# Who evicts the turned normal rows, and where GpSimd's centring stands in its queue, in a fused encoder-decoder kernel

## The chip, the cores and the metric

The kernel runs on one core of a Trainium2 chip. The metric is the device time of one execution in microseconds; the time of a kernel is the median of its runs. A core has a matrix engine (TensorE, in the profile PE, its weight loads PEld), a vector engine (VectorE, DVE), an engine for activation functions (ScalarE, ACT), a general engine (GpSimd, POOL) and one that issues the DMAs here (SyncE, SP). Each engine works through its own queue in program order and waits for the others at semaphores. [...]

## What is computed

One encoder layer over a short context (2 x 77 rows) and one decoder layer over the input (2 x 2048 rows, width 512, 16 heads of 32), both with a normalization ahead of each part. All is in fp32. The reference, cut to the part that matters here:

```python
yn = _ln(y, dec_n1_s, dec_n1_b)                    # (x - mean) * rsqrt(var + eps) * s + b
y = y + _mha(yn, yn, dec_sa_in_w, dec_sa_in_b, dec_sa_out_w, dec_sa_out_b, sb)    # causal, relative bias
y = y + _mha(_ln(y, dec_n2_s, dec_n2_b), memory, ...)                             # cross attention
h = _ln(y, dec_n3_s, dec_n3_b)
y = y + (relu(h @ dec_ff1_w.T + dec_ff1_b) @ dec_ff2_w.T + dec_ff2_b)
```

## The kernel before

The self attention comes first and takes the span up to about 1745 us; cross attention and feed forward of all blocks follow. The self attention goes through 8 blocks of 512 rows (2 sequences, `b`, by 4, `m`). A block has 16 units: 4 groups `g` of 4 heads by 4 tiles `t` of 128 rows. A unit's scores reach over `m * 4 + t + 1` tiles of keys, so units of the first block of a sequence (`m` = 0) are short, and those of the last are long.

For every unit the main loop (lines 1479 to 1504) does this, in program order of all engines: `scores` (L372 on TensorE, the maxima on VectorE in L381 and L388, their combination `nm` in L398, the exponentials on ScalarE in L403), `turn` (L426: TensorE transposes the probabilities into PSUM banks, which L432 on ScalarE and L430 on VectorE copy out), and `values` (L443). Where a unit ends, three lists are worked through for the next unit `n + 1`: first `ahead[n + 1]`, before the last `turn` of unit `n`; after that `turn`, in `slot(n + 1)`, `light`, then the projections of `jobs`, then `late`. The lists are filled by hand in lines 935 to 968. In the first blocks `late` also carries the encoder's stages (L584 to L633), and `light` the first cross attention's stages in the fifth and sixth block (L764 to L853).

The part at hand is the normalization of the rows of the next block, one tile of 128 rows at a time, while a block is worked on:

- `norm_load` (L272) loads the tile.
- `norm_stats` (L277): mean and variance on VectorE (L281 to L284), then 1 / sqrt by GpSimd's power (L285).
- `norm_center` (L288): (x - mean) * rstd in place, on GpSimd (L292), for the very first block on VectorE.
- `norm_turn` (L294): four 128x128 transpositions on TensorE (L304) into one bank, then four evictions that apply scale and bias per partition, into `nT`, from which the next block's `q_job`, `k_job` and `v_job` read. For the first block `apart` is true: two banks, the first quarter evicted by VectorE (L311), the other three by ScalarE (L309). For the other seven blocks, 28 tiles, VectorE evicts all four quarters (L311).

The stages of tile `t` stand at the units 5 + t (load), 6 + t (statistics and centring) and 7 + t (turning) of the block before. In the same slots stand `residual` (a DMA, then GpSimd's add in L266, which waits for it), the stages of `spread` (GpSimd's multiply in L471) and `out_job` (L251 on TensorE, L254 on VectorE, which reads the residual of the unit before). In `light` they come ahead of the centring.

PSUM's banks 0 to 6 are handed out in turn by `bank()`: each user takes the next one, and TensorE's writing waits until the bank's last user, seven requests earlier, has been evicted. Bank 7 collects the values.

Of the kernel before, what the change touches and what calls it, by code (L numbers as in the profile page):

```python
# [54 lines left out]
def tile_encoder_decoder(ctx: ExitStack, tc: tile.TileContext, ins, out):  # L55
# [21 lines left out]
    def vec(name, i):  # L77
        c = _COL[name] + i
        return vecs[:, c : c + 1]
# [78 lines left out]
    with (  # L158
# [20 lines left out]
        def bank():  # L179

            i = count["bank"] % count["banks"]
            count["bank"] += 1
            return psum[:, i, :]
# [27 lines left out]
        def q_job(b, m, g):  # L211
            def run(w):
                mm = bank()
                for c in range(NC):
                    nc.tensor.matmul(mm, w[:, c, :], nTs[b, m][:, c, :], start=(c == 0), stop=(c == NC - 1))
                q = sb.tile([P, MB], F32, name="q", tag="q", bufs=3)
                nc.vector.tensor_scalar(q, mm, vec("dec_sa_in_b", g), SCALE, ALU.add, ALU.mult)
                qTs[b, m, g] = q

            return lambda: small_w(g * P), run, True  # L220

        def k_job(b, m, g):
            def run(w):
                mm = bank()
                for c in range(NC):
                    nc.tensor.matmul(mm, w[:, c, :], nTs[b, m][:, c, :], start=(c == 0), stop=(c == NC - 1))
                d, bi = kT[:, g, ts(m, MB)], vec("dec_sa_in_b", NC + g)
                if m >= 2:
                    nc.vector.tensor_scalar(d, mm, bi, None, ALU.add)
                else:  # L230
                    nc.scalar.activation(d, mm, AF.Identity, bias=bi)

            return lambda: small_w(D + g * P), run, True

        def v_job(b, m, t):
            def run(w):
                mm = bank()
                for c in range(NC):
                    nc.tensor.matmul(
                        mm, nTs[b, m][:, c, ts(t, P)], w[:, c, :], start=(c == 0), stop=(c == NC - 1)  # L240
                    )
                nc.vector.tensor_tensor(vv[:, m * TB + t, :], mm, bv, ALU.add)

            return lambda: big_w("v", b, m), run, False

        def out_job(b, m, t):
            def run(w):
                x1 = xr.pop((b, m, t))
                mm = bank()
                for c in range(NC):  # L250
                    nc.tensor.matmul(  # L251
                        mm, ots[b, m, c][:, ts(t, P)], w[:, c, :], start=(c == 0), stop=(c == NC - 1)
                    )
                nc.vector.tensor_tensor(x1, mm, x1, ALU.add)  # L254
                nc.sync.dma_start(y1[b][m][:, t, :], x1)

            return lambda: big_w("o", b, m), run, False
# [10 lines left out]
        def residual(b, m, t):  # L268
            residual_load(b, m, t)
            residual_add(b, m, t)  # L270

        def norm_load(b, m, t, place=None):  # L272
            x1 = sb.tile([P, D], F32, name="xt", tag="xt", bufs=2) if place is None else place
            nc.sync.dma_start(x1, x_rows[b, m, :, t, :])
            xs[b, m, t] = x1

        def norm_stats(b, m, t):  # L277
            x1 = xs[b, m, t]
            st = sm.tile([P, 6], F32, name="bnst", tag="bnst")
            mv = sm.tile([P, 2], F32, name="bnmv", tag="bnmv")  # L280
            nc.vector.bn_stats(st, x1)  # L281
            nc.vector.bn_aggr(mv, st)
            rs = sm.tile([P, 2], F32, name="rstd", tag="rstd")
            nc.vector.tensor_scalar_add(rs[:, 0:1], mv[:, 1:2], EPS)  # L284
            nc.gpsimd.tensor_tensor(rs[:, 1:2], rs[:, 0:1], mhalf[:, 0:1], ALU.pow)  # L285
            xs[b, m, t] = x1, mv, rs

        def norm_center(b, m, t):  # L288
            x1, mv, rs = xs[b, m, t]
            xs[b, m, t] = x1  # L290
            engine = nc.gpsimd if (b, m) != (0, 0) else nc.vector
            engine.tensor_scalar(x1, x1, mv[:, 0:1], rs[:, 1:2], ALU.subtract, ALU.mult)  # L292

        def norm_turn(b, m, t, apart=False):  # L294
            xn = xs.pop((b, m, t))
            if t == 0:
                nTs[b, m] = nTt
            nT = nTs[b, m]

            pts = [bank()] * NC  # L300
            if apart:
                pts[0] = bank()
            for c in range(NC):
                nc.tensor.transpose(pts[c][:, ts(c, P)], xn[:, ts(c, P)], ident)  # L304
            for c in range(NC):
                d, pt = nT[:, c, ts(t, P)], pts[c]
                sc, bi = vec("dec_n1_s", c), vec("dec_n1_b", c)
                if apart and c:
                    nc.scalar.activation(d, pt[:, ts(c, P)], AF.Identity, bias=bi, scale=sc)  # L309
                else:  # L310
                    nc.vector.tensor_scalar(d, pt[:, ts(c, P)], sc, bi, ALU.mult, ALU.add)  # L311
# [162 lines left out]
        def divide(b, m, g):  # L474


            ri = sm.tile([P, TB, HC], F32, name="ri", tag="ri", bufs=2)
            nc.vector.reciprocal(ri, sums_of[b, m, g])
            rows = sm.tile([P, TB, HC, HD], F32, name="rirows", tag="rirows", bufs=1)
            nc.vector.tensor_copy(rows, ri[:, :, :, None].to_broadcast([P, TB, HC, HD]))  # L480
            yield
            rb = bank()
            flat = rows.rearrange("p t r d -> p (t r d)")
            for t in range(TB):
                nc.tensor.transpose(rb[:, ts(t, P)], flat[:, ts(t, P)], ident)
            nc.vector.tensor_tensor(ots[b, m, g], rb, ots[b, m, g], ALU.mult)
            yield
# [440 lines left out]
        NU = NC * TB  # L928
        jobs = {n: [] for n in range(-1, len(units) + NU)}
        light = {n: [] for n in range(-1, len(units) + NU)}  # L930

        ahead = {n: [] for n in range(-1, len(units) + NU)}
        late = {n: [] for n in light}

        for x, (b, m) in enumerate(blocks):
            u = x * NU
            first = m == 0

            jobs[max(u - 5, -1)].append(q_job(b, m, 0))
            jobs[max(u - 4, -1)].append(k_job(b, m, 0))  # L940
            jobs[(u + 1 if first else u - 3 + (x == 1)) if x else -1].append(v_job(b, m, 0))
            jobs[(u + 2 if first else u - 2 + (x == 1)) if x else 1].append(v_job(b, m, 1))
            jobs[u + 3 if first else u + 1].append(v_job(b, m, 2))
            jobs[u + 4 if first else u + 2].append(v_job(b, m, 3))
            jobs[u - 1 if x else 0].append(q_job(b, m, 1))
            jobs[u if x else 2].append(k_job(b, m, 1))
            for g, at, then in ((2, 3, 4), (3, 5, 6)) if x else ((2, 3, 4), (3, 5, 6)):
                jobs[u + at].append(q_job(b, m, g))
                jobs[u + then].append(k_job(b, m, g))
            for t in range(TB):  # L950
                end = x == len(blocks) - 1
                jobs[u + NU + (2 if end else 7) + t].append(out_job(b, m, t))
                if not end:
                    light[u + NU + 6 + t].append(lambda b=b, m=m, t=t: residual(b, m, t))
                elif t < 2:
                    light[u + NU - 1].append(lambda b=b, m=m, t=t: residual(b, m, t))
                if x:
                    light[u - NU + 5 + t].append(lambda b=b, m=m, t=t: norm_load(b, m, t))
                    ahead[u - NU + 6 + t].append(lambda b=b, m=m, t=t: norm_stats(b, m, t))
                    light[u - NU + 6 + t].append(lambda b=b, m=m, t=t: norm_center(b, m, t))  # L960
                    light[u - NU + 7 + t].append(lambda b=b, m=m, t=t: norm_turn(b, m, t))
            for g in range(NC):
                apart = not (x == len(blocks) - 1 and g >= NC - 2)
                d = spread(b, m, g) if apart else divide(b, m, g)
                for k in range(4 if apart else 2):
                    light[u + g * TB + TB + k].append(lambda d=d: next(d, None))
                at = u + g * TB - 3
                light[max(at, -1)].append(lambda b=b, m=m, g=g: load_bias(b, m, g))
# [197 lines left out]
        u = 2 * NU  # L1166
# [5 lines left out]
        u = 6 * NU  # L1172
# [399 lines left out]
```

## Time and profile before

| what | us |
|---|---|
| median of 3 runs (2849.39 to 2850.22) | 2850.07 |
| the profiled execution's own time | 2851.01 |
| its span, first to last instruction | 2849.2 |
| TensorE busy in the span | 2800.5 |
| VectorE busy | 1888.1 |
| ScalarE busy | 1370.0 |
| GpSimd busy | 836.7 |

The mean granted TensorE clock over the span is 0.994. The profile is of one execution, so the durations of single instructions are set against its own time; the medians are of other executions of the same kernel. How its lines are read: a line of a group has the line of the kernel, the engine, the operation, what it writes and reads, shapes and count, then the busy time, the mean of one in ns, and the idle time of the engine just before them with what ended it. A line of the timeline has start, duration, engine, line, operation, count, and in brackets the idle time before it with its releaser. A line of the windows has the stretch and its length, the busy time of PE, PEld, DVE, ACT and POOL with counts, then the granted clock, the DMAs' busy share and GB/s. The ends of matmuls are modelled, so a busy TensorE isn't TensorE at its peak.

### The profile page before, as it was taken

The page shows a single profiled execution, that of the slowest core. Times are in us where ns is not written, and L with a number is a line of the kernel's source. Part 1 is how long each engine was busy: PE and PEld are TensorE (multiplying, and loading weights), DVE is VectorE, ACT ScalarE, POOL GpSimd, SP SyncE. Part 2 cuts the span into 40 slices and gives each one's busy share as a digit, 9 for nine tenths or more (in the row PEclk, how much of TensorE's full clock was granted, in tenths as well). Part 3 has the DMA queues.
Part 4 walks back from the last instruction along what each step waited for, and adds up shares of the span by engine and source line. Part 5 has one row for each costly group of instructions (what it writes and reads, how often), then busy time and mean ns, then how long its engine had stood idle before and what let it go on. Part 6 is the DMA issues. An engine that isn't in the chain of part 4 may idle for free. (4 is left out here: it accounts for less than half of the span.)

```text
span 2849.2 us, 64689 instructions
## 1 busy us (share of the span) xinstructions
PE 2800.5 (98%) x25662; PEld 2020.5 (71%) x25662; DVE 1888.1 (66%) x5366; ACT 1370.0 (48%) x2583; POOL 836.7 (29%) x695
## 2 busy tenths in 40 slices
PE   9899999999999999999999999999999999999998
PEld 5557666666666456666666677888888888888888
DVE  4766687878886578788778894545454645454545
ACT  3444465546665446555556674333333333333331
POOL 0301143300100302121100002363636363636355
PEclk9899999999999999999999999999999999999999
DMA  6414343401112512232301115454546454545465
GB/s 172 123 46 140 119 140 106 129 23 49 36 50 65 141 39 71 81 106 78 98 20 43 44 34 191 137 178 135 180 136 197 134 181 135 180 135 180 120 203 181
DMA packets 262336, 324.55 MB, mean 114 GB/s; under 512 B 36192, under 2 KB 149392, under 8 KB 261906
## 3 DMA queue, kind: packets, MB, share of 16 engines
q1 hardware_dynamic: 262034, 320.42, 37.4%
q8 instruction: 202, 3.31, 0.5%
q14 instruction: 100, 0.82, 0.1%
HBM read 280.94 MB, written 39.40 MB: 112 GB/s over the span
## 5 line engine op out<-in xcount | busy, mean ns | idle before, releaser
L403 ACT ACTIVATE pp<-pp,nm 128x128 f32<-128x128 f32 (+15 forms) x512 | 611.7, 1201 | 258.9 <-DVE nm L398 258.6
L381 DVE TENSOR_SCALAR_CACHE_REDUCE pp<-psum 128x512 f32<-128x512 f32 (+3 forms) x1024 | 559.6, 591 | 63.1 <-PE psum L372 61.2
L426 PEld LDWEIGHTS psum<-ident,pp 128*128 128x128 f32 x4352 | 475.1, 142 | 106.2 <-DVE pp L381 50.8
L426 PE MATMUL psum<-ident,pp 128*128 128x128 f32 x4352 | 535.0, 278 | 7.0 <-ACT pp L403 3.7
L432 ACT COPY pts<-psum 128x512 f32<-128x512 f32 (+3 forms) x592 | 297.3, 575 | 457.3 <-PE psum L426 343.5
L430 DVE COPY pts<-psum 128x512 f32<-128x512 f32 (+2 forms) x544 | 330.0, 660 | 66.7 <-PE psum L426 66.3
L372 PE MATMUL psum<-kT,q 32*128 32x512 f32 (+3 forms) x2560 | 359.9, 576 | 5.2 <-ACT pts L432 2.6
L443 PEld LDWEIGHTS psum<-pts,vv 128*32 128x32 f32 x8704 | 226.2, 110 | 124.5 <-issue 116.6
L1355 PE MATMUL psum<-pp 128*128 128x128 f32 x2560 | 306.4, 276 | 1.9 <-POOL pp L1113 1.6
L1355 PEld LDWEIGHTS psum<-pp 128*128 128x128 f32 x2560 | 295.8, 192 | 17.4 <-issue 12.6
L443 PE MATMUL psum<-pts,vv 128*32 128x128 f32 x8704 | 279.4, 276 | 0.7 <-ACT pts L432 0.5
L1326 PE MATMUL psum<-vv,pp 128*128 128x256 f32 x1024 | 238.5, 381 | 0.0
L372 PEld LDWEIGHTS psum<-kT,q 32*128 32x128 f32 x2560 | 124.7, 183 | 141.5 <-issue 89.6
L1326 PEld LDWEIGHTS psum<-vv,pp 128*128 128x128 f32 x1024 | 189.8, 190 | 32.2 <-issue 8.4
L388 DVE CUSTOM_DVE_ANT_0 pp<-psum,bias 128x256 f32<-128x256 f32 (+1 forms) x512 | 196.0, 411 | 16.7 <-PE psum L372 16.5
L1113 POOL TENSOR_TENSOR pp<-pp 128x512 f32<-128x512 f32 x124 | 171.1, 1395 | 56.5 <-DMA pp<-in_dec_ff_wT_dram 53.5
L1342 ACT ACTIVATE kT<-kT,vecs 128x256 f32<-128x256 f32 x192 | 86.9, 499 | 192.1 <-DVE kT L1339 192.1
L1339 DVE TENSOR_TENSOR kT<-kT,psum 128x512 f32<-128x512 f32 x96 | 65.7, 685 | 169.8 <-PE psum L1326 96.9
L1326 PE MATMUL psum<-nT,pp 128*128 128x256 f32 x768 | 173.4, 379 | 0.0
L829 POOL TENSOR_TENSOR oT<-oT,cri 128x1232 f32<-128x1232 f32 x28 | 67.7, 2418 | 346.2 <-DVE cri L824 346.2
L1326 PEld LDWEIGHTS psum<-nT,pp 128*128 128x128 f32 x768 | 145.3, 190 | 28.6 <-issue 10.2
L285 POOL TENSOR_TENSOR rstd<-rstd,mhalf 128x1 f32<-128x1 f32 x32 | 18.5, 577 | 486.1 <-DVE rstd L284 424.4
(192 smaller groups left out, 3685.4 us busy)
## 6 DMA issues: line engine op xcount, KB each, us to landing
pp<-w_d SPq DMA_DIRECT2D x520, 256.0 KB
pp<-in_dec_ff_wT_dram SPq DMA_DIRECT2D x112, 256.0 KB
wqk<-in_dec_sa_in_wT_dram SPq DMA_DIRECT2D x64, 256.0 KB
bias<-tzg SPq DMA_DIRECT2D x128, 128.0 KB
wbig<-in_dec_sa_in_wT_dram SPq DMA_DIRECT2D x8, 1024.0 KB
vv<-in_enc_ff_wT_dram SPq DMA_DIRECT2D x8, 1024.0 KB
wbig<-in_dec_sa_out_wT_dram SPq DMA_DIRECT2D x8, 1024.0 KB
vv<-y SPq DMA_DIRECT2D x32, 256.0 KB
```

Of the source, the lines that this page charges most:

```text
L372: nc.tensor.matmul(banks[r][:, : kn * P], q[rows4(r), ts(t, P)], kT[rows4(r), g, k0 * P : (k0 + kn) * P], start=True, stop=True,)
L381: nc.vector.tensor_scalar(p[:, k0 * P : (k0 + far) * P], s[:, : far * P], 1.0, None, ALU.mult, ALU.max, accum_out=st["mx"][:, r, c : c + 1],)
L388: nc.vector.tensor_tensor_reduce(p[:, (i + 1) * P - w : (i + 1) * P], s[:, far * P : kn * P], biases[b, m, g][:, r, 2 * P - w :], 1.0, LOW ...
L403: nc.scalar.activation(p, p, AF.Exp, bias=nm, accum_out=to)
L426: nc.tensor.transpose(pt[:, ts(x, P)], state[n]["p"][r][:, ts(k, P)], ident)
L430: nc.vector.tensor_copy(pts[:, : len(load), :], pt[:, :w])
L432: nc.scalar.copy(pts[:, : len(load), :], pt[:, :w])
L443: nc.tensor.matmul(ot[rows4(r), t, :], vv[:, k, ts(g * HC + r, HD)], got.pop((n, k, r)), start=(k == 0), stop=(k == i),)
L1113: engine.tensor_tensor(out, a, b, ALU.subtract)
L1326: nc.tensor.matmul(mm[:, ts(f, TOK)], a[:, c, ts(f, P)], b[:, c, :], start=fresh and f == 0 and c == 0, stop=c == 1, skip_group_check=True,)
L1342: nc.scalar.activation(dst[:, e, :], src[:, e, :], AF.Relu, bias=vec("dec_ff1_b", f + e))
L1355: nc.tensor.matmul(psum[:, bank_i, ts(col, P)], lhs[:, c, :], w[:, c, :], start=fresh and k in (0, 3) and c == 0, stop=c == 3, skip_group_ ...
```

## The change

Two lines change. In `norm_turn` the choice of the evicting engine is turned round: ScalarE takes a quarter if it isn't the first or if `apart` is false, so that for the 28 tiles of the last seven blocks ScalarE evicts all four quarters, and the first block stays as it is. In the lists `norm_center` of tile `t` goes from `light` to `ahead` of the same unit, right behind `norm_stats`: it is issued before the last `turn` of the unit before instead of after it, and before what else `light` has for GpSimd.

```diff
@@ norm_turn
-                if apart and c:
+                if c or not apart:
                     nc.scalar.activation(d, pt[:, ts(c, P)], AF.Identity, bias=bi, scale=sc)
                 else:
                     nc.vector.tensor_scalar(d, pt[:, ts(c, P)], sc, bi, ALU.mult, ALU.add)
@@ the lists
                     ahead[u - NU + 6 + t].append(lambda b=b, m=m, t=t: norm_stats(b, m, t))
-                    light[u - NU + 6 + t].append(lambda b=b, m=m, t=t: norm_center(b, m, t))
+                    ahead[u - NU + 6 + t].append(lambda b=b, m=m, t=t: norm_center(b, m, t))
                     light[u - NU + 7 + t].append(lambda b=b, m=m, t=t: norm_turn(b, m, t))
```

## The prediction

> **What bounds the kernel now.** I read the page first, then the groups by line for the instructions that the diff touches, then the waits of TensorE in the self attention (0 to 1745 us), then the timeline around all 28 places where a tile of normal rows is turned. Part 1 of the page:
>
> ```profile
> PE 2800.5 (98%) x25662; PEld 2020.5 (71%) x25662; DVE 1888.1 (66%) x5366; ACT 1370.0 (48%) x2583; POOL 836.7 (29%) x695
> ```
>
> TensorE has work or a modelled end of work nearly always, so a microsecond counts only if TensorE was standing for it. The groups by line give the prices of the edit:
>
> ```profile
> L783 ACT ACTIVATE nT<-psum,vecs 128x128 f32<-128x128 f32 x112 | 42.1, 456 | 27.3 <-PE psum L780 27.3
> ...
> L311 DVE TENSOR_SCALAR nT<-psum,vecs 128x128 f32<-128x128 f32 x116 | 39.5, 402 | 2.9 <-PE psum L304 2.7
> ...
> L254 DVE TENSOR_TENSOR xr<-psum,xr 128x512 f32<-128x512 f32 x30 | 20.7, 692 | 44.3 <-PE psum L251 27.8 <-issue 7.7 <-POOL xt L292 3.8
> ...
> L292 POOL TENSOR_SCALAR xt<-xt,bnmv,rstd 128x512 f32<-128x512 f32 x28 | 58.2, 2078 | 0.3
> ...
> L309 ACT ACT_TABLE_LOAD x1 | 1.3, 1283 | 3.7 <-DMA vecs<-in_vecs_dram 3.7
> ```
>
> L783 is the very operation that the edit puts in place of L311: one quarter of a turned tile, scale and bias per partition, by ScalarE. L292 is GpSimd's centring. The waits of TensorE name it once:
>
> ```profile
> PE psum L304 <- POOL xt L292: 3.7, 1, 3.7
> ```
>
> So of 28 centrings 27 came before TensorE asked for them.
>
> **The change part by part.** The first edit moves 112 of L311's 116 instructions (28 tiles, four each) to ScalarE; the other 4, and L309's 12, belong to the first block, where `apart` is true, and stay. VectorE loses 28 groups of 1.36 us; ScalarE gains 28 of 1.50 us (one group of four of each stands in the next fence). No table load comes with it: the trace has a single one, at L309, although L783 and the exponentials alternate.
>
> The second edit puts the centring right behind the power (L285) of the same tile. What it is moved past on GpSimd's queue is the residual's add (L266) and the multiply of `spread` (L471); no DMA is issued by it, and SP's queue is unchanged. Where neither stands between, nothing changes. Where one does, the centring is some 1.3 or 2.5 us earlier, and the adds are 2.08 us later; these are read by `out_job` a unit later, at the least 7 us, so I count this at nothing; without that cover it costs 2.08 us of one L254.
>
> *Term A, the one late centring (unit 72).* The timeline from 950 us:
>
> ```profile
> 951.93 0.56 POOL L285 TENSOR_TENSOR rstd<-rstd,mhalf 128x1 f32<-128x1 f32 x1 [1.70 <-DVE rstd L284]
> ...
> 952.72 1.36 DVE L311 TENSOR_SCALAR nT<-psum,vecs 128x128 f32<-128x128 f32 x4
> ...
> 953.72 0.83 ACT L432 COPY pts<-psum 128x384 f32<-128x384 f32 x2
> 954.44 1.50 ACT L783 ACTIVATE pp<-psum,vecs 128x128 f32<-128x128 f32 x4
> ...
> 955.84 1.97 PE L426 MATMUL psum<-ident,pp 128*128 128x128 f32 x16
> ...
> 956.88 1.27 POOL L266 TENSOR_TENSOR xr<-xr,row_dec_sa_out_b 128x512 f32<-128x512 f32 x1 [4.39 <-DMA xr<-in_x_dram]
> ...
> 959.37 2.07 POOL L292 TENSOR_SCALAR xt<-xt,bnmv,rstd 128x512 f32<-128x512 f32 x1
> ...
> 961.49 1.11 PE L304 MATMUL psum<-ident,xt 128*128 128x128 f32 x4 [3.69 <-POOL xt L292]
> ...
> 962.40 4.58 PE L790 MATMUL psum<-pp,vv 128*128 128x512 f32 x8
> ...
> 972.49 0.60 PE L304 MATMUL psum<-ident,xt 128*128 128x128 f32 x4
> ...
> 972.93 3.60 PE L790 MATMUL psum<-pp,vv 128*128 128x512 f32 x8
> ```
>
> GpSimd finished the power at 952.49, then stood 4.39 us for the residual's DMA with the centring queued behind it. Issued at once, the centring ends at 952.49 + 2.07 = 954.6, and L304 need not wait: 3.69 us. The stand costs more than itself, since the clock drops after it:
>
> ```profile
> 957.00:964.00 7.00, 3.31 (x14) 2.16 (x13) 3.95 (x11) 2.58 (x10) 7.00 (x6) 0.78 0.23 72
> ```
>
> The granted clock (seventh figure) is 0.78 here; L304 and L790 last 1.11 and 4.58 us, against 0.60 and 3.60 ten microseconds later: 0.5 + 1.0 more. Together 5.2 us go. [...]
>
> What is late next? In the same unit ScalarE also evicts a slab of the first cross attention (L783, 954.44). The four new evictions are ahead of it in program order, so it slides from 954.44–955.94 to 955.9–957.5. Its bank is, by counting the ring of seven, the second one that the 16 transpositions at 955.84 want (the first is the turned tile's own, free at 955.95). They need 0.44 us per bank, so the second waits from 956.4 to 957.5 and L304 starts near 958.85, not 957.65. A new stand of 1.2 us: A = −5.2 + 1.2 = **−4.0 us**. Bounds: −5.2 if banks fall otherwise, −2.5 if the clock drops all the same.
>
> *Term B, the first block.* Units are short, VectorE also carries the encoder, and here it is the bound:
>
> ```profile
> 106.34 1.33 DVE L311 TENSOR_SCALAR nT<-psum,vecs 128x128 f32<-128x128 f32 x4
> ...
> 107.58 1.43 DVE L605 TENSOR_REDUCE esu<-pp 77x16 f32<-77x1232 f32 x1
> ...
> 109.21 0.36 DVE L388 CUSTOM_DVE_ANT_0 pp<-psum,bias 128x256 f32<-128x256 f32 x1
> ...
> 109.63 0.33 PE L426 MATMUL psum<-ident,pp 128*128 128x128 f32 x1 [1.37 <-DVE mx L388]
> ...
> 110.89 0.51 ACT L403 ACTIVATE pp<-pp,nm 128x256 f32<-128x256 f32 x1 [3.26 <-DVE nm L398]
> ...
> 112.12 1.36 DVE L311 TENSOR_SCALAR nT<-psum,vecs 128x128 f32<-128x128 f32 x4
> ...
> 113.65 1.65 PE L372 MATMUL psum<-kT,q 32*128 32x384 f32 x4 [1.67 <-ACT pts L432]
> ...
> 117.49 0.62 ACT L403 ACTIVATE pp<-pp,nm 128x384 f32<-128x384 f32 x1 [3.73 <-DVE nm L398]
> ...
> 123.18 0.72 ACT L403 ACTIVATE pp<-pp,nm 128x512 f32<-128x512 f32 x1 [2.67 <-DVE nm L398]
> ...
> 124.86 3.60 PE L215 MATMUL psum<-nT,wqk 128*128 128x512 f32 x8
> ```
>
> VectorE runs without a gap from L311 through L605 to L388, TensorE waits for that L388, ScalarE for the maximum behind it (3.26 us). With L311 gone everything from L388 on is 1.3 us earlier. At 112.12 the same again, up to ScalarE's wait at 117.49; there some 0.2 us are lost, since VectorE then meets TensorE's scores. The third tile gives nothing more: TensorE's own scores set the end. ScalarE's idle times of 3.26, 3.73 and 2.67 us take 1.50 each. So L215 starts 1.3 + 1.1 = 2.4 us earlier. B = **−2.4 us**, between 0 and −4.0 (three groups).
>
> *Term C, the second tile of the third block and its twin.* Rows of 501 us:
>
> ```profile
> 501.40 1.33 DVE L311 TENSOR_SCALAR nT<-psum,vecs 128x128 f32<-128x128 f32 x4
> ...
> 501.99 0.71 PE L372 MATMUL psum<-kT,q 32*128 32x256 f32 x8
> ...
> 502.63 0.69 DVE L254 TENSOR_TENSOR xr<-psum,xr 128x512 f32<-128x512 f32 x1
> ...
> 504.93 1.36 ACT L403 ACTIVATE pp<-pp,nm 128x1280 f32<-128x1280 f32 x1 [6.89 <-DVE nm L398]
> ...
> 507.39 2.10 PE L372 MATMUL psum<-kT,q 32*128 32x512 f32 x7
> ```
>
> L254's products were done when L372 began (501.99), so L254 could start near 502.1 rather than 502.63, and the maximum, the exponential at 504.93 and the copies for which L372 at 507.39 stands come 0.5 us sooner. The twin lies at 1354 us. C = **−1.0 us**, between 0 and −2.7.
>
> *The other 23 tiles: nothing.* Behind L311 stands L254, which waits for TensorE anyway (44.3 us over 30, its row above), so VectorE's 1.36 us become idle time. On ScalarE the group falls into idle time; the tightest place is unit 42's:
>
> ```profile
> 534.34 2.06 ACT L432 COPY pts<-psum 128x512 f32<-128x512 f32 x4 [1.68 <-PE psum L426]
> ```
>
> 1.68 us of idle before it, 1.50 to place. If this cover were gone, it costs up to 1.5 us a tile. [...]
>
> Sum: −4.0 − 2.4 − 1.0 = −7.4 us. The profiled execution took 2851.0 (span 2849.2), so 2843.6; the median, 2850.07, lies 0.9 below it: **2842.7 us**.
>
> **The rivals.**
> 1. *Only the late centring pays* (B and C are swallowed: ScalarE's evictions hold banks that the next scores want). Speaks for it: seven banks, and units in the first block use nine or more. Against: ScalarE's idle rows. 2850.1 − 4.0 = 2846, no measurable change.
> 2. *The stand moves instead of going.* L304 no longer waits for GpSimd, but the bank of L783 is late and then the copies; the clock falls as before. The change does not do what it says, −1 in all: 2849.
> 3. *ScalarE becomes the bound* in the third and seventh block (units 39 to 42 and their twins), where L372 already stands for its copies (507.39). It decides from the point where the group no longer fits into ScalarE's idle time (1.68 us at 534.34). Price 8 × 1.5 = 12, less A: 2858, slower.
> 4. *The clock falls elsewhere.* At 633 us it drops without any tie to this change:
>
> ```profile
> 635.85 4.45 PE L426 MATMUL psum<-ident,pp 128*128 128x128 f32 x20
> ```
>
> 222 ns each, against 123 for the 16 at 955.84. If an earlier start shifts this away, another 20 × 0.1 = 2 us, with B: 2840.
>
> **How the numbers follow.** Forecast 0.50, rivals 0.22, 0.10, 0.12 and 0.06 in order. Some 0.2% (5.7 us, so 2844.4 and 2855.8) is about what a measurement of this kernel can tell from no change; the forecast's own spread, 2839 to 2846 by the bounds of A, B and C, puts 0.06 of its 0.50 above 2844.4. Faster 0.44 + 0.06 = 0.50, same 0.06 + 0.22 + 0.10 = 0.38, slower 0.12. Range 2839 to 2851: all but rival 3 and the forecast's lowest end.
>
> **What would show it.** A: no wait of L304 for L292, and L790 near 962 with 3.6 us; the wait inside the transpositions before it. B: L215 at 122.4 us. C: the exponentials of 504.93 half a microsecond sooner against L254. L311 reduced to 4, L309 at 124. Wrong, if L372's waits for ScalarE's copies grow in the third block, or if TensorE stands before L304 as long as now.

## The result and the profile after

| | before | after |
|---|---|---|
| median (9 runs each), us | 2849.39 (2847.42 to 2851.57) | 2842.48 (2840.56 to 2844.37) |
| profiled execution, us | 2851.01 | 2844.37 |
| its span, us | 2849.2 | 2842.6 |
| VectorE / ScalarE busy, us | 1888.1 / 1370.0 | 1852.4 / 1409.1 |

After to before is 0.9977, with a 95% interval of 0.9967 to 0.9987: 6.9 us less, faster by a little more than can be told from no change. The forecast was 2842.7.

Part 1 of the page, and the groups by line, of the changed kernel:

```profile
PE 2798.0 (98%) x25662; PEld 2020.1 (71%) x25662; DVE 1852.4 (65%) x5254; ACT 1409.1 (50%) x2695; POOL 837.2 (29%) x695
```

```profile
L309 ACT ACTIVATE nT<-psum,vecs 128x128 f32<-128x128 f32 x124 | 46.6, 462 | 6.4 <-PE psum L304 6.4
...
L254 DVE TENSOR_TENSOR xr<-psum,xr 128x512 f32<-128x512 f32 x30 | 20.7, 692 | 69.2 <-PE psum L251 41.4 <-issue 12.9 <-POOL xr L266 7.7
```

112 evictions have gone from L311 to L309, and 36 us of VectorE's time with them. 25 us of that time reappear as idle time ahead of L254 (44.3 us before, 69.2 now): most of VectorE's relief turned into waiting, as expected of the 23 tiles. The 7.7 us that the row puts down to GpSimd's add (L266) aren't a wait for it: at 513.18, 763.64 and 1358.83 us L254 starts 0.1 us after TensorE's last L251, and the add that it reads had ended 11 us or more before.

The waits of TensorE in the changed kernel, cut to what touches the edit:

```profile
PE psum L251 <- DMA wbig<-in_dec_sa_out_wT_dram: 1.0, 1, 1.0
...
PE psum L426 <- ACT pp L783: 0.7, 1, 0.7
```

L304's 3.7 us for GpSimd's L292 are gone; 0.7 us for the slab's eviction (L783) and 1.0 us for a weight load have come. The timeline around unit 72:

```profile
945.77 0.56 POOL L285 TENSOR_TENSOR rstd<-rstd,mhalf 128x1 f32<-128x1 f32 x1 [1.71 <-DMA pp<-tz]
...
946.44 2.07 POOL L292 TENSOR_SCALAR xt<-xt,bnmv,rstd 128x512 f32<-128x512 f32 x1
...
948.29 1.50 ACT L309 ACTIVATE nT<-psum,vecs 128x128 f32<-128x128 f32 x4
949.67 1.51 ACT L783 ACTIVATE pp<-psum,vecs 128x128 f32<-128x128 f32 x4
...
950.03 1.27 POOL L266 TENSOR_TENSOR xr<-xr,row_dec_sa_out_b 128x512 f32<-128x512 f32 x1 [1.52 <-DMA xr<-in_x_dram]
...
951.24 1.53 PE L426 MATMUL psum<-ident,pp 128*128 128x128 f32 x12 [0.74 <-ACT pp L783]
...
952.60 0.60 PE L304 MATMUL psum<-ident,xt 128*128 128x128 f32 x4
...
953.04 3.60 PE L790 MATMUL psum<-pp,vv 128*128 128x512 f32 x8
```

The centring directly follows the power; the add behind it now does the waiting (1.52 us) and holds up nobody. The slab's evictions stand behind the four of the turned tile, and the transpositions wait for their bank. L304 and L790 last 0.60 and 3.60 us, at a granted clock of 1.00 (948 to 957 us).

In the first block:

```profile
106.60 1.50 ACT L309 ACTIVATE nT<-psum,vecs 128x128 f32<-128x128 f32 x4
...
109.20 0.33 PE L426 MATMUL psum<-ident,pp 128*128 128x128 f32 x1 [0.51 <-DVE mx L388]
...
110.47 0.51 ACT L403 ACTIVATE pp<-pp,nm 128x256 f32<-128x256 f32 x1 [1.25 <-DVE nm L398]
...
116.33 0.62 ACT L403 ACTIVATE pp<-pp,nm 128x384 f32<-128x384 f32 x1 [1.60 <-DVE nm L398]
...
122.34 3.60 PE L215 MATMUL psum<-nT,wqk 128*128 128x512 f32 x8
```

The waits for VectorE's maxima fell from 1.37, 3.26 and 3.73 us to 0.51, 1.25 and 1.60, and L215 starts at 122.34, 2.5 us sooner.

TensorE's instructions are the same in both kernels and in the same order, so its two streams can be laid beside each other. The difference of the starts (after less before) stays level over long stretches; where it steps from one level to the next:

| before's time, us | step, us | what is there |
|---|---|---|
| to 125 | −2.5 | first block (term B) |
| 507, 1360 | −0.3, −0.3 | the two tiles of term C |
| 634 to 640 | −2.5 | half clock of before is absent |
| 920 | −0.8 | L215; before waits 0.4 us here for its weights `wqk` |
| 956 | +1.0 | wait for the slab's bank |
| 961 to 964 | −5.2 | the late centring and the clock behind it |
| 1028 to 1033 | +1.3 | half clock twice as long |
| 1487 | +1.9 | half clock that before does not have |
| 1631 | +0.9 | wait for the weights `wbig` |

They add up to −6.5; the streams end 6.6 us apart. Five of the rows are no term of the prediction: 634, 920, 1028, 1487 and 1631. They nearly cancel (+0.8 us).

Granted clocks (seventh figure) of these stretches, first of before, then of after:

```profile
121.00:125.00 4.00, 4.00 (x31) 3.19 (x30) 2.29 (x12) 1.82 (x5) 0.00 (x0) 0.57 0.02 4
633.00:640.00 7.00, 7.00 (x29) 4.96 (x25) 5.42 (x18) 2.42 (x4) 0.00 (x0) 0.52 0.01 2
1028.00:1035.00 7.00, 6.70 (x38) 3.36 (x42) 5.48 (x13) 0.62 (x2) 0.00 (x0) 0.76 0.00 0
```

```profile
104.00:111.00 7.00, 6.38 (x67) 4.65 (x65) 6.08 (x19) 5.67 (x18) 5.72 (x4) 0.86 0.13 42
121.00:125.00 4.00, 4.00 (x23) 2.56 (x20) 2.93 (x15) 1.93 (x5) 0.00 (x0) 1.00 0.02 4
633.00:640.00 7.00, 7.00 (x54) 3.56 (x56) 4.66 (x12) 7.00 (x10) 0.00 (x0) 1.00 0.01 4
948.00:955.00 7.00, 6.18 (x59) 4.09 (x58) 4.47 (x17) 7.00 (x24) 5.38 (x5) 1.00 0.39 127
1017.00:1024.00 7.00, 6.04 (x31) 3.62 (x32) 4.23 (x10) 1.28 (x4) 0.00 (x0) 0.52 0.00 0
1474.00:1482.00 8.00, 8.00 (x33) 5.93 (x32) 6.80 (x27) 1.66 (x4) 0.00 (x0) 0.57 0.01 2
```

Stretches at about half clock are gone from two places (121 and 633 us, 0.57 and 0.52 before, 1.00 after), one has appeared (1474, 0.57), and the one at 1017 (0.52) stands around the instructions of before's at 1029 (0.76), twice as long. Behind the turning at 952 us the clock is 1.00, where before had 0.78. The total is right; the runs below ask whether its terms are.

### The profile page after: what moved, and what is told of

The parts are those of the page before. It is cut to its first block, busy times and chain, and to the rows that moved or that the text cites. A ratio compares the mean times of both kernels' runs of the same rounds, so it can differ in the third digit from the quotient of the medians.

```text
span 2842.6 us, 64681 instructions
## 1 busy us (share of the span) xinstructions
PE 2798.0 (98%) x25662; PEld 2020.1 (71%) x25662; DVE 1852.4 (65%) x5254; ACT 1409.1 (50%) x2695; POOL 837.2 (29%) x695
## 5 line engine op out<-in xcount | busy, mean ns | idle before, releaser
L388 DVE CUSTOM_DVE_ANT_0 pp<-psum,bias 128x256 f32<-128x256 f32 (+1 forms) x512 | 196.0, 411 | 16.8 <-PE psum L372 16.6
```

The lines of the kernel that those rows point to most:

```text
L388: nc.vector.tensor_tensor_reduce(p[:, (i + 1) * P - w : (i + 1) * P], s[:, far * P : kn * P], biases[b, m, g][:, r, 2 * P - w :], 1.0, LOW ...
```

## The experiments

Edits are against the changed kernel unless said otherwise. Median and interval are from the runs beside the kernel before on the same chip; "streams" means the steps of TensorE's starts as above.

| kernel | median, us | before beside it | ratio, 95% interval | span |
|---|---|---|---|---|
| evictions alone | 2842.90 | 2848.84 | 0.9983 (0.9974 to 0.9992) | 2844.7 |
| centring alone | 2845.77 | 2848.84 | 0.9991 (0.9982 to 1.0000) | 2846.8 |
| one tile back on VectorE | 2842.82 | 2848.84 | 0.9980 (0.9971 to 0.9989) | 2842.4 |
| residual's load earlier, nothing else | 2846.64 | 2848.97 | 0.9992 (0.9983 to 1.0001) | 2843.2 |
| earlier load and evictions | 2843.64 | 2848.81 | 0.9981 (0.9972 to 0.9990) | 2839.6 |
| four evictions for one, 8 tiles | 2877.23 | 2848.84 | 1.0103 (1.0089 to 1.0116) | 2874.2 |
| 12 activations beside, 8 tiles | 2849.71 | 2848.97 | 1.0001 (0.9991 to 1.0010) | 2847.3 |
| 28 activations beside, 8 tiles | 2874.84 | 2848.81 | 1.0091 (1.0077 to 1.0105) | 2873.9 |

The theory was the prediction's sum: a late centring (A), VectorE's relief in the first block (B) and in two other tiles (C), and everywhere else ScalarE's idle time as a cover.

**Each half alone.** The evictions without the centring:

```diff
-                    ahead[u - NU + 6 + t].append(lambda b=b, m=m, t=t: norm_center(b, m, t))
+                    light[u - NU + 6 + t].append(lambda b=b, m=m, t=t: norm_center(b, m, t))
```

> Only the evictions go to ScalarE; the centring stays behind the residual. Theory (three separate terms): the late centring of unit 72 stays, so TensorE stands before L304 as before (3.7 us), the slab's late bank hides behind that stand; B and C remain, -3.4 us against the kernel before (ratio 0.9988), TensorE's stream ahead by some 2.4 us at 126 us and 3.5 us at 520 us. Rival (only the late centring pays): no gain, 0 us. Rival (ScalarE is the bound): slower than before, +5 or more.

and the centring without the evictions:

```diff
-                if c or not apart:
+                if apart and c:
```

> Only the centring goes ahead of the residual; VectorE evicts as before. Theory: L304 of unit 72 doesn't wait, and no slab is pushed back, so the whole 5.2 us go there and nothing else moves: TensorE's stream level with before up to 957 us and 5.2 us ahead from 967 us on; ratio 0.9982. Rival (the earlier centring pays in other tiles too): more than 6 us. Rival (the stand moves): less than 2 us.

Measured: −5.9 us for the evictions and −3.1 for the centring, by medians; each is uncertain by some 2.7 us. The centring's kernel did in its streams what was expected of the edit: nothing in the first block (−0.01 at L215 near 125 us), and −5.3 us at 961 to 964. Steps that were not expected gave part back: +1.0 at 920 (a wait of 1.4 us for the weights `wqk`), +0.8 at 1029 and +1.5 at 1631. The evictions' kernel did not: the stall at unit 72 should have stayed, and it shrank. Its waits:

```profile
PE psum L251 <- DMA wbig<-in_dec_sa_out_wT_dram: 3.1, 1, 3.1
...
PE psum L304 <- POOL xt L292: 0.4, 1, 0.4
```

and GpSimd's rows there:

```profile
942.74 0.76 SPq L262 DMA_DIRECT2D xr<-in_x_dram  x1
945.08 0.47 PEld L304 LDWEIGHTS psum<-ident,xt 128*128 128x128 f32 x4
...
949.64 1.28 POOL L266 TENSOR_TENSOR xr<-xr,row_dec_sa_out_b 128x512 f32<-128x512 f32 x1 [2.18 <-DMA xr<-in_x_dram]
```

The add waits 2.18 us for the residual and not 4.39, since SP issued the load 2.3 us ahead of the weights of unit 71's turning (L304), not 0.7 us as in the first profile of before. The streams step by −3.6 us there, though the centring is where it was. Either the evictions do this, or it differs from execution to execution. Both kernels were therefore profiled again, unchanged.

> The kernel before, unchanged, for a second profile. Theory (order and waits are fixed): L304 of unit 72 waits 3.7 us again within half a microsecond, and the clock falls at 633, 961 and 1029 us again. Rival (the waits for DMAs and the clock's drops differ from one execution to the next): the wait differs by more than 1 us, or a drop comes at another place.

> The changed kernel, unchanged, for a second profile. Theory: L304 of unit 72 doesn't wait, the transpositions before it stand 0.7 us for the slab, out_job at 1625 us waits about 1.0 us for its weights, and the clock falls at 1017 and 1475 us. Rival (execution by execution): the last two differ by more than 1 us or come at another place.

The second execution of the kernel before (2849.78 us, span 2847.9; the changed one 2842.55, span 2840.8) shows, first its SP and GpSimd, then its waits:

```profile
935.51 9.01 SPq L112 DMA_DIRECT2D pp<-tz  x8
...
945.47 0.76 SPq L262 DMA_DIRECT2D xr<-in_x_dram  x1
947.38 0.47 PEld L304 LDWEIGHTS psum<-ident,xt 128*128 128x128 f32 x4
...
952.47 1.28 POOL L266 TENSOR_TENSOR xr<-xr,row_dec_sa_out_b 128x512 f32<-128x512 f32 x1 [2.71 <-DMA xr<-in_x_dram]
```

```profile
PE psum L304 <- POOL xt L292: 2.0, 1, 2.0
PE psum L251 <- DMA wbig<-in_dec_sa_out_wT_dram: 1.6, 1, 1.6
```

The kernel is the same, and its stall is 2.0 us instead of 3.7. In the first profile:

```profile
938.70 9.71 SPq L112 DMA_DIRECT2D pp<-tz  x8
...
949.43 0.79 SPq L262 DMA_DIRECT2D xr<-in_x_dram  x1
950.11 0.47 PEld L304 LDWEIGHTS psum<-ident,xt 128*128 128x128 f32 x4
```

There the load had 0.7 us of lead over L304's weights, here 1.9: the eight loads (L112) ahead of it in SP's queue took 9.71 us there and 9.01 here, and began 0.5 us later by TensorE's stream (which is 2.7 us ahead here). The add then began 7.45 us after its load's issue there, 7.00 here. Together that is 1.6 of the 1.7 us between the stalls. By the same reckoning the evictions' kernel (lead 2.3 us, add after 6.90) would have a stall of some 1.5 us; its 0.4 is what is left of that behind a wait of 0.7 us for the slab's bank, which comes ahead of it there too. From the power's end to the add's start, the lateness of the load is 4.39 us in the first profile and 2.2 to 3.8 us in the nine other profiles that have the load at its old place. So the prediction read the longest lateness of ten, and term A isn't one number.

The drop of the clock at 633 us is absent in the second execution as well (1.00 from 633 to 640); the one behind the stall is there, at 958.2 us. In the second execution of the changed kernel L304 doesn't wait and the waits for the slab (0.7 us) and for `wbig` (1.1 us) are back as expected, and the drop of 1475 us is absent (1.00 from 1475 to 1481). Laid beside each other, the two executions of the kernel before differ by −2.5 us at 634, −0.6 at 920, +1.0 at 1029 and +1.6 at 1631, and those of the changed kernel by −2.0 at 1480. So each of the five steps that are no term also comes or goes with no edit at all.

The second pair of executions has almost nothing but the terms: −3.4 us in the first block, −0.3 and −0.3 at the tiles of C, +1.0 for the slab's bank, −3.9 for the late centring and its clock, and −0.2 for all the rest. Its streams end 7.1 us apart.

**What makes the centring late.** If the cause is the add ahead of it, which waits for a DMA, an earlier DMA does as well as an earlier centring. Against the kernel before, with evictions and centring as they were:

```diff
-                    light[u + NU + 6 + t].append(lambda b=b, m=m, t=t: residual(b, m, t))
+                    light[u + NU + 6 + t - (t == 1)].append(lambda b=b, m=m, t=t: residual_load(b, m, t))
+                    light[u + NU + 6 + t].append(lambda b=b, m=m, t=t: residual_add(b, m, t))
```

> The kernel before, with the load of the residual's second tile issued one unit earlier (with the first tile's, ahead of the eight loads of the cross attention's table), its add where it was. The evictions stay on VectorE, the centring stays behind the add. Theory (the centring is late because the add ahead of it waits for a load that stood in SP's queue): the add doesn't wait, L304 of unit 72 isn't late, -5.2 us as with the centring moved, to the same stream at 967 us. Rival (something else holds GpSimd): L304 waits as before, 0 us.

```profile
949.83 0.56 POOL L285 TENSOR_TENSOR rstd<-rstd,mhalf 128x1 f32<-128x1 f32 x1 [1.70 <-DVE rstd L284]
950.35 1.28 POOL L266 TENSOR_TENSOR xr<-xr,row_dec_sa_out_b 128x512 f32<-128x512 f32 x1
...
952.85 2.08 POOL L292 TENSOR_SCALAR xt<-xt,bnmv,rstd 128x512 f32<-128x512 f32 x1
...
955.54 0.60 PE L304 MATMUL psum<-ident,xt 128*128 128x128 f32 x4
```

The add still stands ahead of the centring and waits for nothing; L304 neither. The streams step by −5.3 us at 961 to 964, as if the centring had been moved. That settles the cause of the late centring. The median gives −2.3 us, with an interval from −4.8 to +0.3, which holds the step of the second pair (−3.9) and not that of the first (−5.2).

This kernel also tells something of term B. With VectorE's work untouched, its L215 starts at 123.58 us, 1.3 sooner than before (0.5 of it are already there at 95 us, 0.8 come in the first block), and the windows show a reason:

```profile
121.00:125.00 4.00, 4.00 (x36) 2.45 (x33) 3.26 (x16) 1.57 (x5) 0.00 (x0) 1.00 0.02 4
```

The half clock of 121 us is absent here too.

**The wait that was added.** The first of the four tiles that are turned in the fifth block back on VectorE, so that the slab's evictions don't slide:

```diff
-                if c or not apart:
+                if (c or not apart) and (b, m, t) != (1, 1, 0):
```

> The changed kernel, with one tile of the 28 given back to VectorE: the first that is turned in the fifth block, unit 71, where ScalarE's slab waits behind it. Theory: the 0.74 us that the transpositions of unit 71 stand for L783 go, about -1.0 us against the changed kernel, -8 against before; the wait of L426 for L783 is gone from the trace. Rival (the bank's wait is hidden or comes from something else): no difference to the changed kernel.

In the streams the step of +1.0 us at 956 is gone (−1.1 at 951 against the changed kernel), so the wait is what the prediction said it would be. In the time nothing is left of it: 2842.82 against 2842.48. One microsecond is below what these medians tell apart. The same edit with the earlier load in place of the moved centring:

> The centring where it was, the residual's load of the second tile one unit earlier, ScalarE's evictions but for the tile beside the slab's. Theory (the terms are: the load's lateness, 5.2 where the stall is as long as in the first profile and 2 where it is short; the first block 2.4; the third and seventh 1.0): L304 doesn't wait for L292 and no new stand comes at 956, about 2849 - 7 to - 8.6 = 2840.5 to 2842, the changed kernel's time within its uncertainty. Rival (the centring must be moved for the gain): no better than the evictions alone, 2843 or more, with a wait of L304 for L292 in the trace.

L304 doesn't wait for L292, and against the changed kernel the streams step by −1.1 us at 951, where its wait for the slab's bank was. 2843.64 us, within the uncertainty of the changed kernel, though above the 2840.5 to 2842 that were expected. No version tried beats it measurably.

**What covers the moved work.** Three kernels load ScalarE in the third and seventh block, where the changed kernel's timeline leaves ScalarE 3.0, 4.3, 4.1 and 0.4 us of idle time in the units of the four tiles (39 to 42), and the same in their twins. First each eviction there four times:

```diff
-                    nc.scalar.activation(d, pt[:, ts(c, P)], AF.Identity, bias=bi, scale=sc)
+                    for _ in range(4 if m == 3 else 1):
+                        nc.scalar.activation(d, pt[:, ts(c, P)], AF.Identity, bias=bi, scale=sc)
```

> The changed kernel, with each of ScalarE's evictions made four times over (the same values written again) for the 8 tiles that are turned in the third and seventh block: 4.5 us more of ScalarE per tile, 36 us in all. Theory (idle time covers it up to its own length: 3.0, 4.3, 4.1 and 0.4 us in the four tiles of a block): 1.5 + 0.2 + 0.4 + 4.1 = 6.2 us a block, +12 us against the changed kernel. Rival (ScalarE is the bound there already): all of it, +36 us. Rival (ScalarE is nowhere near): 0.

Measured: 34.8 us more than the changed kernel, three times the expected 12. TensorE's waits in the third block (lines are one higher here: L427 transposes, L310 evicts, L404 is the exponential):

```profile
489.39 6.03 PE L427 MATMUL psum<-ident,pp 128*128 128x128 f32 x28 [3.29 <-ACT nT L310]
509.27 2.84 PE L427 MATMUL psum<-ident,pp 128*128 128x128 f32 x24 [1.81 <-ACT nT L310]
524.35 3.28 PE L427 MATMUL psum<-ident,pp 128*128 128x128 f32 x28 [1.89 <-ACT nT L310]
546.28 5.04 PE L427 MATMUL psum<-ident,pp 128*128 128x128 f32 x29 [5.80 <-ACT pp L404]
```

Three waits name the eviction: the turned tile's bank was held. Is it the bank, then, and not ScalarE's time? Behind the four evictions, 12 activations from SBUF to SBUF (a copy in place), which hold no bank:

```diff
+            for c in range(3 * NC if m == 3 else 0):
+                d = nT[:, c % NC, ts(t, P)]
+                nc.scalar.activation(d, d, AF.Identity, scale=1.0)
```

> The changed kernel with 12 more instructions of ScalarE behind the evictions of the same 8 tiles (each writes a quarter of the evicted tile over itself, SBUF to SBUF, three times round): again about 4.5 us per tile, but the bank is free after the first four. Theory (in the run with the evictions made four times the waits of the transpositions for the evictions' bank, 14.0 us, came on top of those for the exponentials, 15.3 against 3.7 us): only the second part is left, +12 us against the changed kernel. Rival (ScalarE's time itself is what counts): +32 as there. Rival (only the bank counts): below 3.

7.2 us more than the changed kernel by the medians, where 12 were expected. TensorE waits at the fourth tile alone, 2.3 us, and 2.3 at its twin; the streams step by 2.4 and 3.8 us there, the latter 1.5 us more than its wait. That looked like the bank. But the two loads are not equal, as two rows of ScalarE show, of the four-for-one kernel and of this one:

```profile
537.40 7.37 ACT L310 ACTIVATE nT<-psum,vecs 128x128 f32<-128x128 f32 x16
```

```profile
527.93 1.49 ACT L309 ACTIVATE nT<-psum,vecs 128x128 f32<-128x128 f32 x4
529.30 2.51 ACT L314 ACTIVATE nT<-nT 128x128 f32<-128x128 f32 x12
```

Twelve more evictions took 7.37 − 1.49 = 5.9 us, twelve activations from SBUF 2.5 (2.4 by their end). So the count was raised from 12 to 28 (`7 * NC`), 5.7 us a tile:

> The extra of 12 activations from SBUF lasted only 2.51 us a tile, that of 12 more evictions 5.9 us (16 in 7.39 against 4 in 1.50). Here 28 activations from SBUF, at 0.21 each 5.8 us a tile, behind the four evictions of the eight tiles of the third and seventh block; the turned tile's bank is free as early as in the changed kernel. Theory (ScalarE's idle time is the cover, whatever holds it up): each unit pays the extra less its idle time of 3.0, 4.3, 4.1 and 0.4 us, so 2.8 + 1.5 + 1.7 + 5.4 = 11.4 a block, 23 in both, about 2865 to 2872 with the clock, near the kernel with four times the evictions (2877). Rival (the held bank made most of that cost): only the last unit pays, as with 12 activations, now 5.4 a block, 11 in both, about 2853 to 2857.

2874.84 us, 32.4 more than the changed kernel and above the expected 2865 to 2872, with no bank held longer. Its waits in the third block:

```profile
489.41 0.66 PE L429 MATMUL psum<-ident,pp 128*128 128x128 f32 x4 [2.06 <-ACT pts L435]
509.06 2.56 PE L375 MATMUL psum<-kT,q 32*128 32x512 f32 x8 [0.69 <-ACT pts L435]
542.32 6.16 PE L429 MATMUL psum<-ident,pp 128*128 128x128 f32 x29 [5.49 <-ACT pp L406]
```

| tile of the third block | ScalarE's idle time, us | four for one: extra less idle | TensorE's wait | 28 beside: extra less idle | TensorE's wait |
|---|---|---|---|---|---|
| first | 3.0 | 2.9 | 3.3 | 2.6 | 2.1 |
| second | 4.3 | 1.6 | 1.8 | 1.3 | 0.7 |
| third | 4.1 | 1.8 | 1.9 | 1.5 | 0 |
| fourth | 0.4 | 5.5 | 5.8 | 5.2 | 5.5 |
| sum | | 11.8 | 12.8 | 10.6 | 8.3 |

(Extra: 5.9 and 5.6 us, the latter as the activations overlap the last eviction by 0.1.) The extra less the idle time carries most of both columns of waits, so ScalarE's idle time was the right cover to look at, but for the third tile: there 1.5 us were due without a held bank, and none came. What had failed in the first expectation was the duration of an added eviction, and the clock was left out. The bank plays a part in the first three tiles only: 1.2, 1.1 and 1.9 us between the two columns of waits, of which 0.3 each are the longer extra.

Their equal totals mislead, by the way. The streams end 31.6 us (four for one) and 31.3 us (28 beside) behind the changed kernel's; twice the sums of the table are 25.6 and 16.6. The rest, some 6 and 15 us, is by estimate mainly the clock: over the span it is 0.991 and 0.989 against 0.994 of the changed kernel, which over 2874 us is some 9 and 14 us. It is low at the first and the fourth tile's wait: 0.57 from 488 to 496 us and 0.52 from 543 to 550 with four for one, and with 28 beside 0.57 from 542 to 549 and, at the first wait:

```profile
489.00:497.00 8.00, 7.59 (x80) 5.24 (x84) 3.22 (x9) 5.53 (x10) 0.00 (x0) 0.57 0.01 2
```

## Why the prediction was right, and where only its sum was

**Term A (−4.0).** In the first pair of profiles −5.2 + 1.0 = −4.2: the wait gone, the clock behind it restored (0.78 to 1.00), and the predicted wait for the slab's bank in its place. The cause is shown twice, by moving the centring alone and by moving the load alone. The size is what was not: 3.69 us were read from one execution as if every run had them, and the second profile has 2.03, with a drop of the clock behind it all the same (at 958.2 us), 3.9 us in all. The step that failed is "3.69 us … Together 5.2 us go", as a term for a median; in the second pair A is −3.9 + 1.0 = −2.9. Centring alone gave 3.1 us in the medians, and on top of the evictions 0.4 (1.0 with each set against the kernel before beside it); neither can be told from the 2.9 or the 4.2 of the profiles with an uncertainty of 2.7.

**Term B (−2.4).** L215 came 2.5 us sooner. The step "everything from L388 on is 1.3 us earlier" holds in itself: the stream goes from 0.7 us behind to 0.4 ahead between 106 and 110 us. The 0.7 were lost just before, since half clock fell on the same stretch (0.86 from 104 to 111, 0.99 before). Another 0.7 came by 120. The last 1.2 us came where the half clock of 121 us is absent (0.57 before, 1.00 after, from 121 to 125), which the sum did not hold. From 95 us to the end of the first block the eight profiled executions with ScalarE's evictions gain 2.2 to 3.4 us on the first profile of before; the three others with VectorE's lose 0.2, gain nothing and gain 0.8. So the evictions do it, and some 0.8 us can come without them. With VectorE's work untouched the half clock of 121 us was absent once in four profiled kernels or executions (1.00 from 121 to 125 with the earlier load, 0.50 to 0.73 in the halves of that stretch in the others), and in each of the eight with ScalarE's evictions (1.00): likely, not shown, that the evictions displace it.

**Term C (−1.0).** −0.3 and −0.3, in both pairs: the right tiles, two thirds of the size. The exponential of 504.93 is at

```profile
501.96 1.36 ACT L403 ACTIVATE pp<-pp,nm 128x1280 f32<-128x1280 f32 x1 [4.30 <-DVE nm L398]
```

2.97 us sooner, of which 2.5 are the first block's. So it comes the forecast 0.5 us sooner, and 0.3 of that stay in TensorE's stream.

**The other 23 tiles (nothing).** Right: no step at any of them, VectorE's time became idle time ahead of L254, and the cover named for ScalarE is the one that the three loaded kernels bear out. By their table the fourth tile of the third and seventh block is the only one of these eight where another half microsecond would have cost. The 2.08 us by which the adds come later cost nothing, as forecast.

**The rivals.** The first (only the centring pays) falls with the evictions alone, 0.9983. The second (the stand moves) falls: 1.0 us came for 5.2. The third (ScalarE becomes the bound) falls: 2.5 us more of ScalarE a tile cost something at two of the eight tiles only. The fourth was right that the clock would move at 633 us, and wrong that this is the edit's gain: −2.5 there, +1.3 and +1.9 elsewhere, and the second executions show each of these steps without any edit.

**The total.** That the sum meets the median within 0.5 us is in part luck: A's size differs by 1.3 us between the two pairs and C's is smaller, B's is up to 1 us larger, and in the first pair the five steps that no term has nearly cancel. The bounds of A, B and C add up to −2.5 and −11.9, which is 2838 to 2848; the 2839 to 2846 given as the forecast's own spread are narrower.

**Not foreseen:** the wait for `wbig` at 1631 us, 0 to 3.1 us in the profiles. An earlier stream isn't what makes it: in all twelve profiles SP issued the load 5.2 to 5.5 us before TensorE came to it. The load's own time differs, up to 8.5 us with the evictions alone, whose streams lost 4.5 us there of the 8.9 that they were ahead, 1.4 more than the wait of 3.1. With the earlier load and the evictions the streams were 9.7 us ahead, and the wait was 0.2 us.

The terms don't add across kernels: 5.9 + 3.1 = 9.0 against 6.9 together. With these uncertainties that isn't a contradiction; the evictions' kernel was profiled with a short stall, which may be its execution's and not its own. This stays open, as does what places the drops of the clock.

## What to carry to other kernels

A stall that stands in one profile is a sample (3.7 us here, 2.0 in the same kernel's second profile): before it becomes a term of a sum, ask what sets its length, and if it is a DMA behind others in a queue, profile the same kernel again. An operation that waits for a DMA, placed ahead of one that doesn't on the same engine, cost the second one the wait here (GpSimd stood 4.39 us, TensorE behind it 3.69); bringing the load forward and changing the order of the two gave the same step here (−5.3 us each). Cover is counted per place, as idle time of the engine that takes the work on, with the added operation's duration as it is when it runs there (5.9 us here for twelve evictions, where 4.5 were reckoned, and 2.5 for twelve copies), and not from a sum over the span.

## What the runs showed of the hardware beyond expectation

In the traces of before and after, the stretches at a granted clock of 0.50, but for the one that ends after the program, have lengths of 3.41, 6.83 or 10.24 us, that is 3.41 times one, two or three: before at 97.4 (6.83), 111.0 (6.83), 121.3 (3.41), 633.3 (6.83), 960.9 (3.41) and 1029.2 us (3.41), after at 95.7 (10.24), 112.8 (6.83), 1017.3 (6.83) and 1474.7 (6.83). Within each of the two executions their starts lie multiples of 3.413 us apart: before, 633.3 − 97.4 is 157.0 times 3.413 and 1029.2 − 97.4 is 273.0 times; after, 1017.3 − 95.7 is 270.0 times and 1474.7 − 95.7 is 404.0 times. The program's instructions alone don't place them: by TensorE's stream after's at 1017.3 starts 1.6 us ahead of before's at 1029.2, and the one at 633.3 is absent from the same kernel's second execution (1.00 from 633 to 640). That a stream which moves by a microsecond or two is cut at other places for that reason would fit, and was not shown.

An idle TensorE doesn't stand ahead of every drop. Ahead of the drop at 960.9 us it is busy for 0.3 of 3.4 us, and in the second execution, ahead of that at 958.2, for 1.4 of 3.4. But at 633.3 us TensorE is shown busy (with modelled ends) for all of the 3.41 us ahead of the drop and all of the 6.83 us of half clock.

An activation of 128x128 fp32 took ScalarE different times: 1.50 us for four evictions from PSUM into four places, 0.46 us each for 16 that write each place four times running, 0.20 us each for the copies from SBUF (28 in 5.70 us). The evictions also read scale and bias per partition and the copies do not, so the runs don't show that the place read from makes the difference.
